# A one-column exponential on ScalarE ahead of each step's scores, in the second phase of a two-block transformer kernel

## The chip, the cores and the metric

The kernel runs on one core of one Trainium2 chip. The metric is the device time of one execution in microseconds (us). The kernel before was run three times: 3278.76, 3273.80 and 3276.89 us, with a median of 3276.89 us. One further execution was profiled.

The engines are named as in the profile: PE is TensorE's matmuls and PEld its weight loads, DVE is VectorE, ACT is ScalarE, POOL is GpSimd and SP is SyncE, which here only issues transfers.

## The reference, cut to what matters

The input is x of shape 8 x 1024 x 256 in float32. Two residual blocks follow each other; the second one has two layers.

```python
x = x + latent_attention(layernorm(x), ...)     # 16 heads, causal, rotary: first phase
x = x + local_blocks(layernorm(x), ...)         # second phase, DEPTH = 2 layers

# one layer of the second phase
h = shift_token(x)
q, k, v = split(h @ wqkv)                       # 8 heads of 64
q, k = rotary_xpos(l2norm(q) * qs, l2norm(k) * ksc)
x = x + softmax(window_mask(8 * q @ k.T)) @ v @ wo   # window 128: own block and the one before
h = layernorm(shift_token(x)) * lg + lb
a, g = split(h @ w1 + b1)                       # 682 columns each
x = x + (a * gelu(g)) @ w2 + b2
```

The scores need an exponential and the MLP needs a Gelu. Both are computed on ScalarE.

## The kernel before, in words

The first phase (`mla`) takes about the first 985 us and computes the latent attention of all 8 batches. It isn't touched by the change. The second phase (`local`) runs 16 passes, one for each layer and batch, layer 0 of all batches first. A pass consists of 8 windows of 128 tokens for the attention and of 2 chunks of 512 tokens for the MLP.

The second phase is a software pipeline written out by hand. The loop at line 1210 makes one step for each window, 128 of them and 11 more to drain. Inside `manual_schedule` each engine executes its instructions in the order in which the code issues them. In step s the loop issues, in this order:

- `both` of window s-4: the sums of masked exponentials of two blocks, on DVE.
- `qk` of window s: the projection to q and k on PE into a PSUM tile "pair" (line 892, recorded as L670 like all that goes through `times`), its squares on ACT (L897), and the rotary work on DVE and POOL (L899 to L912).
- `transposes` of window s-1: a transpose on DVE, a write to DRAM (z) and a read back into qkT through SP's queue (L930 to L939).
- `v` of window s: the projection to the values on PE ("pv", L670) and its eviction by ACT (L79).
- the first unit of the MLP (line 1227), from step 11 on.
- `values` of window s-4: the weighted values ("o", L1003) and the sums ("s", L1011) on PE, then the division on DVE.
- `scores` of window s-3: in two halves of four heads. Each half has its matmuls on PE into a "pair" tile (L962), an exponential of that tile on ACT (L968) into "pt", and masks on POOL (L970, L975).
- `output`, in every second step: the output projection on PE ("psw", L670).
- the second unit of the MLP (line 1238).

There are two "pair" tiles in PSUM, taken in turn (`turns`, line 869). A step takes three: one for `qk` and one for each half of the scores. The tile that `qk` of the next step writes is therefore the one that the first half's exponential of this step reads.

The MLP is a generator whose units the loop draws one at a time. A chunk has 8 units, so it spans 4 steps. Five units consist of a gate and a value projection ("ag", L670), a Gelu on ACT (L1127) and a product on DVE (L1128). The sixth does the remaining columns: half as many matmuls, a Gelu at L1137, and two products at L1142. The seventh is the down projection ("psy", L670), and the eighth only scales the next chunk's input on ACT (L1091). With two units a step the sixth is always the second unit of its step, and what follows it on PE is `qk` of the next step.

ScalarE keeps the table of one set of functions at a time, and exponential and Gelu belong to different sets. The compiler puts an ACT_TABLE_LOAD ahead of an activation that needs the other set; it is recorded under that activation's line. In the kernel before, the wait for PE that belongs to the first exponential of a step stands on the table load in 116 of its 120 cases. The other four are three loads without any wait, in the steps just after the change from layer 0 to layer 1, and one that waits for DVE, later on.

Of the kernel before, what the change touches and what calls it, by code (L numbers as in the profile page):

```python
# [29 lines left out]
F32 = mybir.dt.float32  # L30
F32R = mybir.dt.float32r
AF = mybir.ActivationFunctionType
# [4 lines left out]
P = 128  # L37
# [45 lines left out]
def preln_mla_local_kernel(  # L83
# [27 lines left out]
    nc = tc.nc  # L111
# [44 lines left out]
    def mla(ctx: ExitStack, verdict):  # L156
# [453 lines left out]
        ALONE = 1 + max(step for step, what in beside.items() for who, name, _ in what if who == 0 and not name.startswith("out"))  # L610
        E = mybir.EngineType
        line, done, turning = [], [], []
        with tc.manual_schedule(engines={E.PE, E.DVE, E.Activation, E.Pool}):
            for b in range(B + 1):
# [43 lines left out]
    def local(ctx: ExitStack, verdict):  # L658
# [4 lines left out]
        p1 = ctx.enter_context(tc.tile_pool(name="l1", bufs=1))  # L663
# [31 lines left out]
        def load_attention(l):  # L695


            w = {}
            queue = nc.sync if l else nc.scalar
            w["qkv"] = wa.tile([P, 2, 3 * INNER], F32, tag="qkv", name=f"l_qkv{l}")  # L700
            nc.sync.dma_start(w["qkv"], wqkv[l].rearrange("(c p) e -> p c e", p=P))

            for name, src in (("cos", xpos_cos), ("sin", xpos_sin)):
                w[name] = wa.tile([P, NT, 2, DH], F32, tag=name, name=f"l_{name}{l}")
                queue.dma_start(w[name], src)
                f = wa.tile([P, 2, DH], F32, tag=f"f{name}", name=f"l_f{name}{l}")
                for i, sc_ in enumerate((q_scale, k_scale)):
                    if name == "cos":
                        queue.dma_start(f[:, i, :], sc_[l].partition_broadcast(P))
                    else:  # L710
                        queue.dma_start(f[:, i, :H], sc_[l, H:].partition_broadcast(P))
                        queue.dma_start(f[:, i, H:], sc_[l, :H].partition_broadcast(P))
                w[f"f{name}"] = f
            return w

        def scale_tables(w):
            for name in ("cos", "sin"):
                f = w[f"f{name}"].unsqueeze(1).to_broadcast([P, NT, 2, DH])
                nc.vector.tensor_tensor(w[name], w[name], f, ALU.mult)

        def load_o(l):

            w = wa.tile([P, 4, D], F32, tag="o", name=f"l_o{l}")
            for g in range(2):
                for j in range(4):
                    h = 4 * g + j
                    nc.sync.dma_start(
                        w[32 * j : 32 * j + 32, 2 * g : 2 * g + 2],
                        wo[l, h * DH : (h + 1) * DH].rearrange("(a p) e -> p a e", a=2),
                    )  # L730
            return w
# [451 lines left out]
        windows = len(passes) * NT  # L1183
        streams = {}

        def ahead(n):
            if n < len(passes):
                l, b = passes[n]
                if n not in streams:
                    streams[n] = stream(b, l)  # L1190
                return next(streams[n])
# [10 lines left out]
        def each(step, name, back):  # L1202
            j = step - back
            if 0 <= j < windows:
                n, i = divmod(j, NT)
                getattr(made[n], name)(i)

        E = mybir.EngineType
        with tc.manual_schedule(engines={E.PE, E.DVE, E.Activation, E.Pool}):
            for step in range(windows + LAG):  # L1210
                n, i = divmod(step, NT)
                if step < windows and i == 0:
                    l, b = passes[n]
                    if n and b == 0:
                        o = w["o"]
                        w = load_attention(l)
                        w["o"] = o
                    made[n] = Pass(n, l, b, w, *ready.pop(n))
                late = step < windows and n and i == 0 and b == 0
                each(step, "both", 4)  # L1220
                if not late:
                    each(step, "qk", 0)
                each(step, "transposes", 1)
                if not late:
                    each(step, "v", 0)
                if step >= LAG:
                    next(units, None)
                if NT - 2 <= i and step < windows:
                    ahead(n + 1)
                each(step, "values", 4)  # L1230
                each(step, "scores", 3)
                j = step - 6
                if 0 <= j < windows and j % 2 == 0:
                    made[j // NT].output(j % NT // 2)
                elif 0 <= j < windows - 1 and (j + 1) % (B * NT) == 0:
                    w["o"] = load_o(passes[(j + 1) // NT][0])
                if step >= LAG - 2:
                    next(units, None)
                if late:
                    scale_tables(w)  # L1240
                    each(step, "qk", 0)
                    each(step, "v", 0)
                if i >= NT - 5 and step < windows:
                    got = ahead(n + 1)
                    if got:
                        ready[n + 1] = got
            for _ in units:
                pass
# [524 lines left out]
    with ExitStack() as two:  # L1773
        local(two, verdict)
# [4 lines left out]
    column = const.tile([P, 1], F32, name="column")  # L1779
# [84 lines left out]
```

## Time and profile before

| what | us |
|---|---|
| median of three runs | 3276.89 |
| the profiled execution, its own time | 3275.27 |
| its span, first to last instruction | 3273.5 |
| first phase, up to about | 985 |
| the second phase fills, about | 985 to 1120 |
| second phase, steady part | 1120 to 3195 |
| drain of the last chunks | 3195 to 3273.5 |

Busy time of the engines by stretch, in us:

| stretch | length | PE | DVE | ACT | POOL |
|---|---|---|---|---|---|
| first phase | 985.0 | 930.94 | 866.75 | 785.88 | 88.72 |
| filling | 135.0 | 109.26 | 110.76 | 38.76 | 103.43 |
| steady part | 2075.0 | 2067.54 | 1665.21 | 874.15 | 1147.22 |
| drain | 78.5 | 69.46 | 28.37 | 13.70 | 2.23 |

A row of the instruction groups reads: line, engine, operation, written tile, read tiles, shape, count, then the busy time and the mean of one in ns, then the idle time of the engine ahead of the group and what ended it. "issue" means that nothing that the profile shows was waited for. The end of a matmul is modelled, its start is recorded. In the weight loads' rows, idle time is usual: the loads come in groups of four, with 0.30 us between groups when matmuls of 512 columns run without a stop.

### The profile page before, as it was taken

The page shows a single profiled execution, that of the slowest core. Times are in us where ns is not written, and L with a number is a line of the kernel's source. Part 1 is how long each engine was busy: PE and PEld are TensorE (multiplying, and loading weights), DVE is VectorE, ACT ScalarE, POOL GpSimd, SP SyncE. Part 2 cuts the span into 40 slices and gives each one's busy share as a digit, 9 for nine tenths or more (in the row PEclk, how much of TensorE's full clock was granted, in tenths as well). Part 3 has the DMA queues.
Part 4 walks back from the last instruction along what each step waited for, and adds up shares of the span by engine and source line. Part 5 has one row for each costly group of instructions (what it writes and reads, how often), then busy time and mean ns, then how long its engine had stood idle before and what let it go on. Part 6 is the DMA issues. An engine that isn't in the chain of part 4 may idle for free.

```text
span 3273.5 us, 112729 instructions
## 1 busy us (share of the span) xinstructions
PE 3177.2 (97%) x50274; PEld 1456.0 (44%) x50274; DVE 2671.1 (82%) x3934; ACT 1712.5 (52%) x2055; POOL 1341.6 (41%) x1064
## 2 busy tenths in 40 slices
PE   7999999999987999999999999999999999999998
PEld 2434343443333445444445444444554444544454
DVE  4999989998987888887888877777877878787773
ACT  6888888888852343444443444444444444444441
POOL 1001000000018655565555555555555555555540
PEclk9999999999998999999999999999999999999999
DMA  4133223323333444544445445444544545454431
GB/s 128 43 95 85 56 75 78 85 53 81 98 98 104 108 129 118 142 111 122 131 115 135 120 131 144 120 130 142 144 131 130 133 122 134 134 140 126 114 106 59
DMA packets 389900, 364.21 MB, mean 111 GB/s; under 512 B 158703, under 2 KB 337310, under 8 KB 389278
## 3 DMA queue, kind: packets, MB, share of 16 engines
q1 hardware_dynamic: 387422, 354.51, 40.1%
q8 instruction: 397, 6.50, 0.8%
q10 hardware_dynamic: 1984, 2.41, 0.2%
q14 instruction: 97, 0.79, 0.1%
HBM read 165.96 MB, written 140.51 MB: 94 GB/s over the span
## 4 chain that ended last, share of the span: by engine, by line
PE 84%; DVE 6%; ACT 4%; DMA 3%; issue 2%; SPq 1%; POOL 0%; ACTq 0%; DVEq 0%; POOLq 0%
PE ag L670 17%; PE pair L670 13%; PE psy L670 9%; PE psw L670 7%; PE acc L488 7%; PE pv L670 6%; PE o L1003 6%; PE sc L455 5%; PE pair L962 4%; DVE pt L477 3%; PE s L1011 2%; PE psx L201 2%; PE psq L201 1%; PE psR L201 1%; ACT pt L463 1%
## 5 line engine op out<-in xcount | busy, mean ns | idle before, releaser
L477 DVE TENSOR_TENSOR pt<-pt,er 128x1024 f32<-128x1024 f32 x576 | 671.9, 1222 | 35.5 <-ACT pt L463 35.5
L670 PE MATMUL ag<-d,l 128*32 128x512 f32 x5632 | 639.8, 593 | 0.7 <-ACT d L1085 0.4
L906 POOL TENSOR_TENSOR t<-t,t 128x1024 f32<-128x1024 f32 x128 | 304.2, 2377 | 780.2 <-DVE t L902 780.2
L463 ACT ACTIVATE pt<-sc 128x1024 f32<-128x1024 f32 x576 | 561.0, 1032 | 115.4 <-PE sc L455 105.6
L968 ACT ACT_TABLE_LOAD x120 | 154.0, 1283 | 686.9 <-PE pair L962 686.8
L670 PE MATMUL pair<-l_qkv,xT 128*32 128x512 f32 x4096 | 468.3, 597 | 6.6 <-ACT pt L968 3.2
L126 POOL TENSOR_TENSOR rn<-ss,half 128x16 f32<-128x16 f32 x128 | 373.4, 2917 | 13.9
L488 PE MATMUL acc<-pt,v 128*32 128x512 f32 (+3 forms) x3072 | 345.6, 497 | 11.1 <-DVE pt L477 10.0
L670 PEld LDWEIGHTS ag<-d,l 128*32 128x32 f32 x5632 | 179.0, 110 | 384.0 <-issue 362.0
L897 ACT ACTIVATE sq<-pair 128x1024 f32<-128x1024 f32 x128 | 131.2, 1025 | 331.0 <-issue 256.0
L899 DVE TENSOR_TENSOR t<-pair,l_cos 128x1024 f32<-128x1024 f32 x128 | 156.3, 1221 | 155.1 <-ACT sq L897 154.8
L670 PE MATMUL psy<-l,hid 128*32 128x256 f32 x5120 | 282.1, 379 | 0.0
L670 PEld LDWEIGHTS pair<-l_qkv,xT 128*32 128x32 f32 x4096 | 132.6, 111 | 307.8 <-issue 252.5
L1128 DVE SCALAR_TENSOR_TENSOR hid<-ag,l_b,ge 128x512 f32<-128x512 f32 x160 | 115.9, 724 | 188.2 <-ACT ge L1127 164.5
L968 ACT ACTIVATE pt<-pair 128x1024 f32<-128x1024 f32 (+1 forms) x256 | 235.1, 969 | 56.4 <-PE pair L962 55.1
L912 POOL TENSOR_TENSOR t<-t,rn 128x1024 f32<-128x1024 f32 x128 | 245.4, 1918 | 10.0
L455 PE MATMUL sc<-q,k 32*128 32x512 f32 (+3 forms) x3072 | 245.2, 380 | 4.0 <-ACT pt L463 3.0
L1003 PEld LDWEIGHTS o<-pt,v 128*32 128x32 f32 x7680 | 212.8, 110 | 72.7 <-issue 68.9
L670 PE MATMUL pv<-l_qkv,xT 128*32 128x512 f32 x2048 | 244.1, 592 | 0.0
L670 PE MATMUL psw<-l_o,oT 128*32 128x256 f32 x4096 | 240.2, 386 | 0.1
L1003 PE MATMUL o<-pt,v 128*32 128x128 f32 x7680 | 235.6, 273 | 1.7 <-POOL pt L970 1.6
L420 POOL TENSOR_SCALAR_AFFINE_SELECT er<-er 128x128 f32<-128x128 f32 x64 | 39.1, 610 | 480.7 <-ACT er L418 480.7
(324 smaller groups left out, 4639.5 us busy)
## 6 DMA issues: line engine op xcount, KB each, us to landing
z<-turned SPq DMA_DIRECT2D x512, 128.0 KB, 2.8
qkT<-z SPq DMA_DIRECT2D x128, 512.0 KB, 3.9
y<-xs SPq DMA_DIRECT2D x128, 128.0 KB, 3.8
h<-y SPq DMA_DIRECT2D x32, 512.0 KB, 4.4
zx<-turneds SPq DMA_DIRECT2D x120, 128.0 KB, 2.8
xT<-zx SPq DMA_DIRECT2D x240, 64.0 KB, 2.9
zh<-turnedh SPq DMA_DIRECT2D x120, 128.0 KB, 2.3
d<-zh SPq DMA_DIRECT2D x30, 512.0 KB, 3.3
```

The source lines that it names most:

```text
L126: nc.gpsimd.tensor_tensor(out_, in_, half[:, :n], ALU.pow)
L455: nc.tensor.matmul(two[n // 2][:, n % 2, lo : lo + w], k[rows], q[rows, h], start=(h == 1), stop=(h == 0),)
L463: nc.scalar.activation(pt, sc, AF.Exp, scale=SCALE)
L477: nc.vector.tensor_tensor(t, t, er.to_broadcast([P, 1024 // w, w]), ALU.mult)
L488: nc.tensor.matmul(self.acc[g][32 * n : 32 * n + 32, q0 - c * 512 :], self.v[:, kb, h * VW : h * VW + 32], pts[n // 2][:, n % 2, lo : lo + w],
L670: nc.tensor.matmul(out[four], w[:, four], rhs, start=start, stop=stop)
L897: nc.scalar.activation(sq, qk, AF.Square)
L899: nc.vector.tensor_tensor(t1, qk, A[:, i].unsqueeze(2).to_broadcast([P, 2, HEADS, DH]), ALU.mult)
L906: nc.gpsimd.tensor_tensor(t1, t1, t2, ALU.add)
L912: nc.gpsimd.tensor_tensor(t1, t1, rn.unsqueeze(3).to_broadcast([P, 2, HEADS, DH]), ALU.mult)
L968: nc.scalar.activation(pt[:, :, : n * P], flat[:, :, : n * P], AF.Exp, scale=-1.0)
L1003: nc.tensor.matmul(o[32 * j : 32 * j + 32, g, a, :], vs[m][:, h * DH + a * 32 : h * DH + a * 32 + 32], pts[m][g][:, place(j), off : off + ...
```

## The change

Two tiles of one column are made ahead of the loop: `column`, which POOL sets to zero, and `spark`. In each step that has scores, a single ACT instruction is issued between the weighted values and the scores: the exponential of `column` into `spark`. Nothing reads `spark`.

```diff
@@ -1205,6 +1205,10 @@
                 n, i = divmod(j, NT)
                 getattr(made[n], name)(i)
 
+        column = p1.tile([P, 1], F32, name="column_l")
+        nc.gpsimd.memset(column, 0.0)
+        spark = p1.tile([P, 1], F32, name="spark")
+
         E = mybir.EngineType
         with tc.manual_schedule(engines={E.PE, E.DVE, E.Activation, E.Pool}):
             for step in range(windows + LAG):
@@ -1228,6 +1232,8 @@
                 if NT - 2 <= i and step < windows:
                     ahead(n + 1)
                 each(step, "values", 4)
+                if 0 <= step - 3 < windows:
+                    nc.scalar.activation(spark, column, AF.Exp)
                 each(step, "scores", 3)
                 j = step - 6
                 if 0 <= j < windows and j % 2 == 0:
```

## The prediction

> **What bounds the kernel now.** I read the page first, then the busy time by stretch, the chain of work that ended last around one chunk boundary, and the timelines of TensorE, its weight loads and ScalarE at two boundaries that differ in one thing.
>
> From the page: the busy shares, and the group that the change is about.
>
> ```profile
> PE 3177.2 (97%) x50274; PEld 1456.0 (44%) x50274; DVE 2671.1 (82%) x3934; ACT 1712.5 (52%) x2055; POOL 1341.6 (41%) x1064
> L968 ACT ACT_TABLE_LOAD x120 | 154.0, 1283 | 686.9 <-PE pair L962 686.8
> ```
>
> TensorE bounds the kernel. ScalarE loads the exponential's table 120 times, 1.28 us each, and nearly always it first sits idle until TensorE has finished the scores (686.8 us of waiting): the load comes after the wait, not during it. The busy time by stretch for the second phase's steady part (columns: stretch, its length, then busy time of PE, PEld, DVE, ACT, POOL, the granted clock and DMA):
>
> ```profile
> 1120.00:3195.00 2075.00, 2067.54 (x36870) 1000.66 (x36864) 1665.21 (x2628) 874.15 (x941) 1147.22 (x851) 1.00 0.47 127
> ```
>
> By this TensorE idles 7.5 us of 2075 us, but ends of matmuls are modelled, so a short stall can hide under a "busy" matmul. The chain shows one. At a chunk boundary (start, length, what):
>
> ```profile
> 1848.77 0.50 ACT L968
> 1849.27 0.79 issue
> 1850.06 1.03 ACT pt L968
> 1851.10 0.04 issue
> 1851.14 3.64 PE pair L670 x32
> ```
>
> The path leaves TensorE, goes through the load (0.50 + 0.79 = 1.29 us) and one exponential (1.03 us), and comes back to the next window's q and k. That matmul group writes the PSUM tile which the first exponential of the step before reads; there are two such tiles and three uses a step. What stands between is only the second half of the scores and whatever the MLP's second unit gives TensorE. In most steps that is 3.4 us or more. In the step with the small remainder unit it is 16 matmuls, and this is what happens (timeline of TensorE; start, length):
>
> ```profile
> 1849.09 1.92 PE L670 MATMUL ag<-d,l 128*32 128x512 f32 x16
> 1851.14 3.64 PE L670 MATMUL pair<-l_qkv,xT 128*32 128x512 f32 x32
> 1854.60 0.61 PE L670 MATMUL pv<-l_qkv,xT 128*32 128x512 f32 x4
> ```
>
> The profile holds a boundary without the late load. In one step just after the layer change the load carries no wait, so ScalarE did it right behind the Gelu, 2.65 us before the scores were ready:
>
> ```profile
> 2272.51 0.69 ACT L1127 ACTIVATE ge<-ag,l_b 128x512 f32<-128x512 f32 x1 [1.13 <-PE ag L670]
> 2273.22 1.28 ACT L968 ACT_TABLE_LOAD   x1
> 2277.16 1.94 ACT L968 ACTIVATE pt<-pair 128x1024 f32<-128x1024 f32 x2 [2.65 <-PE pair L962]
> ```
>
> and TensorE there, same unit, same order:
>
> ```profile
> 2277.52 1.92 PE L670 MATMUL ag<-d,l 128*32 128x512 f32 x16
> 2279.26 3.62 PE L670 MATMUL pair<-l_qkv,xT 128*32 128x512 f32 x32
> 2282.70 0.61 PE L670 MATMUL pv<-l_qkv,xT 128*32 128x512 f32 x4
> ```
>
> From the first remainder matmul to the first of the values' projection it is 5.51 us with the late load (1849.09 to 1854.60) and 5.18 us with the early one (2277.52 to 2282.70): 0.33 us, of which 0.31 is the stall and 0.02 the weight load that could not be pulled ahead. Is it kept? The down projections of successive chunks, by the timeline of TensorE:
>
> ```profile
> 1224.34 8.82 PE L670 MATMUL psy<-l,hid 128*32 128x256 f32 x160
> 1294.05 6.23 PE L670 MATMUL psy<-l,hid 128*32 128x256 f32 x112
> ...
> 2215.04 8.81 PE L670 MATMUL psy<-l,hid 128*32 128x256 f32 x160
> 2284.41 5.79 PE L670 MATMUL psy<-l,hid 128*32 128x256 f32 x104
> ```
>
> The chunk with the stall lasts 69.71 us and the one without 69.37 us. The 0.33 us was not handed back within the chunk.
>
> **What the Trainium skill says.** "ScalarE: Activation LUTs", section "What ACT_TABLE_LOAD costs", gives about 1283 ns for a load, which the trace repeats exactly, and a drain of about 1380 ns on top, which it does not show: the Gelu's load at 1852.02 starts 0.02 us after the exponential's end, and the exponential starts 11 ns after its load. I take 1.28 + 0.01 us. "Perfetto Trace Analysis", section "Tensor Engine Instruction (MATMUL, LD_WEIGHTS)", says the end of a TensorE instruction is an estimate; hence I count from start to start. "TensorE: Matmul & The Clock Gate", section "Step-by-step: what each phase is for", says weights are pulled ahead of running matmuls; here the early boundary loads them at 2278.84, 0.42 us ahead of their matmul, the late one at 1851.14 together with it.
>
> **The change part by part.** *The load moves.* The instruction order of the changed kernel has the same 120 exponential loads and 121 Gelu loads; the 120 stand ahead of the one-column exponential and carry no wait, and the wait for TensorE is on the first real exponential. No other engine's order changes, except for one more memset on POOL before the loop. So a load starts when ScalarE gets there: after the values' eviction or the first unit's Gelu. Apart from the four loads that ran early, the shortest idle time before a load is 3.1 us, so load and one-column exponential fit before the scores are ready in every step.
>
> *The cost of the one-column exponential.* No row has this shape. The rotary exponentials of line 418 take 293 ns for 128 columns and 617 ns for 512, that is 0.84 ns a column and 186 ns fixed: 0.19 us. The skill's ScalarE section gives the same 186 ns with immediate scale and bias. 128 of them are 24 us on an engine busy 874 of 2075 us, in idle stretches of at least 3.1 us: 0 us on the path. Eight come before the first Gelu and bring no load; ScalarE is busy 39 of 135 us there. Were the cover gone, 0.19 us in 28 steps would be 5 us. Its wait is for its own predecessor's write, a step earlier: nothing.
>
> *What is gained.* The first exponential ends about 1.3 us earlier. The stall was 0.33 us, so it goes whole: the chain would have the tile free at 1848.77 + 1.03 + 0.04 = 1849.84, while TensorE wants weights at about 1850.41 (one group of four 0.43 us after the load at 1849.98). 0.57 us to spare. Where such a boundary stands: 32 chunks, of which the last three have no later q and k: 29, less the early one: 28. The waits say the same:
>
> ```profile
> PEld pair L670 <- ACT pt L968: 37.0, 54, 1.3
> ```
>
> 54 waits in the steady part; an ordinary one between groups of four weight loads is 0.30 us and a stalled one 1.03: 1.03 n + 0.30 (54 - n) + 0.28 = 37.0 gives n = 28, where 0.28 is the surplus of one longer stall (1.31 us, at 2209.86). The sum: 27 x 0.33 + 0.60 = 9.5 us. Nothing in the other steps: with a full unit or an output projection between, TensorE does not wait for an exponential. The second Gelu of a step and the mask on POOL also come 1.3 us earlier, into engines that wait for others. What is late next: once, shortly before the layer change, TensorE waits 2.8 us for the q/k transfer, and that chain starts from TensorE's own output, so it moves along.
>
> Against its own time: span 3273.5 - 9.5 = 3264.0, and with the 1.8 us around it 3265.8. The profiled execution (3275.27) lies 1.6 us under the median, 3276.89; so 3267.4 us, -0.29%. I count 0.2% (6.6 us) as about what a measurement can tell from no change.
>
> **The rivals.** *The gain is handed back* (no change, 3275 to 3277): TensorE arrives 0.33 us earlier at something that has its own clock, a transfer or VectorE (busy 80% there). For it: VectorE's share. Against: the 69.37 us chunk. *The larger reading* (3256): the weight loads' idle is 1.03 instead of 0.30 us, so 0.73 x 28 = 20 us. Against: the loads are normally pulled ahead, so most of this is lost lead, and start to start it is 0.33. *Slower* (above 3283.5): every tile allocated later in the two working pools lies 64 bytes further on. If a q/k round trip got longer by this, the place is the 2.8 us wait and its like at the 15 changes of pass, where SyncE's queue holds the stream's transfers ahead; it decides from 9.5 + 6.6 = 16 us in all, 1.1 us a change. Against: every row keeps its length and size; unknown otherwise, so from 0 to 16 us, and I take 0. *It does not do what it says* (3277 to 3282): the exponential still starts 1.3 us behind the scores, 0 to 5 us lost to the extra instruction; the order of instructions speaks against it.
>
> **How the numbers follow.** Forecast 0.76, handed back or not working 0.14, larger 0.05, slower 0.05. The forecast itself spans 8.5 to 10 us of gain, and the three runs before span 5 us: 3264 to 3271. With a part of the handed-back case and of the larger one I take 3263 to 3274. Faster by over 0.2% (below 3270.3): nearly all of the first (0.71) and the larger case, 0.76; within 0.2%: 0.18; slower: 0.06.
>
> **What would show it.** Table loads on the new line, 120 of them, with no wait for TensorE, and no idle time left that is ended by TensorE ahead of a load of the exponential; the first remainder matmul to the first of the values' projection 5.18 us at every boundary; chunks of 69.37 and 70.5 instead of 69.7 and 70.86 us; the weight loads' wait for the exponentials near 8 us in place of 37.0. The prediction is wrong if these hold and the end does not move (handed back), if boundaries keep 5.5 us, or if the wait for the q/k transfer grows.

## The result, and the profile after

Over 16 runs of each kernel the changed kernel takes 3267.6 us (median; 3265.09 to 3272.61) and the kernel before 3275.38 us (3273.72 to 3279.6). The ratio is 0.9977, with a 95% interval of 0.9969 to 0.9984: 7.8 us faster, where 9.5 us were forecast. The interval reaches from 5.2 to 10.2 us, so the times alone can't tell these two apart; the traces below can. Two repeats beside other experiments gave 0.9979 (0.9970 to 0.9988) and 0.9981 (0.9974 to 0.9989).

The table loads, first. This is the view of instruction groups on ScalarE between 1120 and 3195 us of the changed kernel (busy time, mean ns, then the idle time ahead and what ended it):

```profile
L968 ACT ACTIVATE pt<-pair 128x1024 f32<-128x1024 f32 (+1 forms) x238 | 218.3, 968 | 523.6 <-PE pair L962 523.6
L1236 ACT ACT_TABLE_LOAD x119 | 152.7, 1283 | 2.1
L1236 ACT ACTIVATE spark<-column_l 128x1 f32<-128x1 f32 x119 | 24.1, 203 | 1.4
```

The wait for the scores is now ahead of the exponential. The loads, as many and as long as before, have 2.1 us of idle time ahead of them in all: they run when ScalarE gets there. At a chunk boundary it looks like this (timeline of ScalarE, changed kernel):

```profile
1844.72 0.69 ACT L1127 ACTIVATE ge<-ag,l_b 128x512 f32<-128x512 f32 x1 [1.13 <-PE ag L670]
1845.43 1.28 ACT L1236 ACT_TABLE_LOAD   x1
1846.72 0.20 ACT L1236 ACTIVATE spark<-column_l 128x1 f32<-128x1 f32 x1
1849.43 1.02 ACT L968 ACTIVATE pt<-pair 128x1024 f32<-128x1024 f32 x1 [2.50 <-PE pair L962]
```

and on TensorE:

```profile
1849.73 1.92 PE L670 MATMUL ag<-d,l 128*32 128x512 f32 x16
1851.48 3.62 PE L670 MATMUL pair<-l_qkv,xT 128*32 128x512 f32 x32
1854.91 1.90 PE L670 MATMUL pv<-l_qkv,xT 128*32 128x512 f32 x16
```

ScalarE has 2.50 us left over after load and extra exponential. From the remainder unit's first matmul to the first of the values' projection it is 5.18 us, where the kernel before had 5.51. By the same starts it is 5.17 to 5.18 us at all 29 boundaries of the changed kernel; before, it was 5.51 us at 27 of them, 5.79 at one and 5.17 at the early one. The weight loads' wait for the exponentials, 37.0 us in the steady part before, is gone there; over the whole program this remains:

```profile
PEld pair L670 <- ACT pt L968: 4.6, 4, 2.2
```

all of it in the filling stretch, before the first unit of the MLP, when no such unit lies between the scores and the next q and k.

Then the chunks, each taken from the first matmul of one down projection to that of the next. Here are three successive down projections in layer 0 (timeline of TensorE, changed kernel):

```profile
1226.27 8.82 PE L670 MATMUL psy<-l,hid 128*32 128x256 f32 x160
1295.64 8.82 PE L670 MATMUL psy<-l,hid 128*32 128x256 f32 x160
1366.50 3.85 PE L670 MATMUL psy<-l,hid 128*32 128x256 f32 x68
```

One chunk lasts 69.37 us, 0.34 less than the same chunk before. The other lasts 70.86 us, as long as before; the same two down projections in the kernel before:

```profile
1294.05 8.82 PE L670 MATMUL psy<-l,hid 128*32 128x256 f32 x160
1364.91 8.82 PE L670 MATMUL psy<-l,hid 128*32 128x256 f32 x160
```

In layer 1 both kinds are shorter where nothing else delays them (69.71 to 69.37, 70.79 to 70.46). So in six chunks of layer 0 the gain was handed back, and the profile names the place. TensorE and VectorE in the second chunk, changed kernel:

```profile
1307.73 1.35 PE L962 MATMUL pair<-qkT 64*32 64x160 f32 x64
1309.38 2.99 PE L670 MATMUL psw<-l_o,oT 128*32 128x256 f32 x49 [0.30 <-DVE xs L1165]
```

```profile
1306.22 1.32 DVE L909 TENSOR_SCALAR ss<-ss 128x16 f32<-128x16 f32 x1
1307.46 1.29 DVE L930 STREAM_TRANSPOSE turned<-t 128x512 f32<-128x512 f32 x2
1308.68 1.24 DVE L1165 TENSOR_TENSOR xs<-psy,xs 128x512 f32<-128x512 f32 x2
1309.86 1.04 DVE L794 TENSOR_SCALAR xs<-xs,mvs,rstds 128x256 f32<-128x256 f32 x3
```

The output projection (psw) needs a PSUM bank, of which the pool has three in turn; the down projection's is the next one, and VectorE frees it with the first addition at L1165. No row on VectorE shows an idle time ahead: it works without a gap from the step's beginning (the rows between 1291 and 1311 us follow each other at 0.035 us or less). In these steps it also normalises the stream of a later pass (the row of L794), which the program does in layer 0 alone; that this is what fills VectorE is read from the rows and was not tried.

Before the change TensorE came to this point just ahead of VectorE. Its output projection began 1.32 us after the scores, and begins 1.65 us after them now:

```profile
1306.14 1.32 PE L962 MATMUL pair<-qkT 64*32 64x160 f32 x64
1307.46 3.66 PE L670 MATMUL psw<-l_o,oT 128*32 128x256 f32 x64
```

The waits for L1165 over the whole program (total us, times, longest), the first row from the kernel before, the other two from the changed one:

```profile
PEld psw L670 <- DVE xs L1165: 1.9, 6, 0.3
PEld psw L670 <- DVE xs L1165: 3.9, 6, 0.7
PE psw L670 <- DVE xs L1165: 1.9, 6, 0.3
```

So the projection's weight loads waited for VectorE in the same six places before, 0.32 us each. TensorE now comes 0.33 us earlier, and they wait 0.33 us longer.

### The profile page after: what moved, and what is told of

It is laid out like the page before. It is cut to its first block, busy times and chain, and to the rows that moved or that the text cites. A ratio compares the mean times of both kernels' runs of the same rounds, so it can differ in the third digit from the quotient of the medians.

```text
span 3267.4 us, 112857 instructions
## 1 busy us (share of the span) xinstructions
PE 3171.2 (97%) x50274; PEld 1460.1 (45%) x50274; DVE 2673.8 (82%) x3934; ACT 1734.9 (53%) x2183; POOL 1341.1 (41%) x1065
## 4 chain that ended last, share of the span: by engine, by line
PE 56%; DVE 4%; issue 1%; DMA 0%; SPq 0%; ACT 0%; DVEq 0%
PE ag L670 16%; PE pair L670 11%; PE psy L670 7%; PE psw L670 6%; PE pv L670 5%; PE o L1003 5%; PE pair L962 4%; PE s L1011 1%; DVE turned L930 0%; DVE rs L1015 0%; DVE bnsts L783 0%; DVE t L902 0%; DVE both L987 0%; DVE turnedh L804 0%; SPq L850 0%
## 5 line engine op out<-in xcount | busy, mean ns | idle before, releaser
L1015 DVE RECIPROCAL rs<-s 128x256 f32<-128x256 f32 x128 | 222.8, 1741 | 13.0 <-PE s L1011 13.0
```

The lines of the kernel that those rows point to most:

```text
L1015: nc.vector.reciprocal(rs, s)
```

## The experiments

Each is compared with the kernel before, run on the same chip in the same rounds. Chunk lengths are worked out from the starts of down projections, as above.

**Only the boundaries.** The instruction is issued in the remainder steps alone:

```diff
-                if 0 <= step - 3 < windows:
+                if 0 <= step - 3 < windows and step >= LAG and step % 4 == 1:
                     nc.scalar.activation(spark, column, AF.Exp)
```

> The one-column exponential is issued only in the steps whose second MLP unit is the small remainder unit (steps 13, 17, ... 129: 30 instead of 128); everywhere else the table load stays behind the scores. Theory (only the 28 boundaries with 16 matmuls of cover mattered): the whole gain, 7.8 us below before, and chunks of 69.37 us in layer 0; some 90 loads with the wait for TensorE stay and cost nothing. Rival (earlier exponentials help in every step, through POOL's masks or VectorE's products): a third or less of the gain, below 3 us.

Measured: 3270.66 against 3277.82 us, ratio 0.9980 (0.9974 to 0.9987). Undisturbed chunks are 69.37 and 70.46 us (70.86 in layer 0), as in the changed kernel. The late loads are still there in numbers (waits of this kernel: total us, times, longest):

```profile
ACT L968 <- PE pair L962: 569.6, 87, 12.2
```

87 loads behind the scores, and the gain is 7.2 us against the changed kernel's 7.8, which the intervals don't tell apart. The boundaries carry the gain.

**All but the boundaries.** The part of the condition that the last experiment added, negated.

> The opposite half: the one-column exponential in every step with scores except the remainder steps. Theory: the stalls of 0.33 us at 28 boundaries stay, chunks of 69.7 and 70.86 us, 0 us against before (within 1.5 us). Rival (gain in all steps): 5 us or more below before.

Measured: 3278.0 against 3277.82 us, ratio 1.0000 (0.9992 to 1.0009), chunks of 69.71 and 70.86 us in layer 0. Its waits for the exponentials and for L1165:

```profile
PEld pair L670 <- ACT pt L968: 31.4, 31, 1.0
PEld psw L670 <- DVE xs L1165: 1.9, 6, 0.3
```

The stalls are there, and the six waits for L1165 are as short as in the kernel before. The 98 extra exponentials and 90 early loads change nothing. With the first experiment this settles where the gain is.

**An instruction without a table.** `AF.Identity` in place of `AF.Exp`; the one-column tile is then copied instead of exponentiated, and nothing reads it.

> The same one-column instruction in the same place, but an identity, which needs no table of its own: the load stays with the first real exponential of each step. It has the same tiles, so the same shift of the later tiles by 64 bytes, and the same count of instructions. Theory (the place of the load is all there is): 0 us against before, within 1.5 us, 116 loads with their wait for TensorE, 0.33 us stalls. Rival (the shift of the tiles, or the order of waits on ScalarE, made the gain): the gain of 7.8 us stays. If the instruction itself cost time on the path: up to 5 us above before.

Measured: 3278.8 against 3277.82 us, ratio 1.0003 (0.9994 to 1.0011). Its waits:

```profile
ACT L968 <- PE pair L962: 674.3, 116, 12.0
PEld pair L670 <- ACT pt L968: 42.0, 59, 2.6
```

These are nearly the rows of the kernel before (686.8 us, 116 times; 41.6 us, 59 times). The program makes the same tiles in the same order and as many instructions as in the changed kernel, so it is the place of the load that counts.

**How much cover there is.** Eight exponentials in place of one, and then twenty in the remainder steps and one elsewhere:

```diff
                 if 0 <= step - 3 < windows:
-                    nc.scalar.activation(spark, column, AF.Exp)
+                    for _ in range(8):          # second kernel: 20 if step >= LAG and step % 4 == 1 else 1
+                        nc.scalar.activation(spark, column, AF.Exp)
```

> Eight one-column exponentials in place of one, 0.2 to 0.26 us each[...], where the shortest idle stretch is 3.1 us and 4.0 us at the boundaries that stall. Theory (the cost is hidden while it fits, and the boundary has 0.57 us to spare): the time of the changed kernel within 1.5 us. Rival (the instruction costs something on the path each time): 0.2 us x 7 x 28 = 39 us or more above.

> The changed kernel with 20 one-column exponentials, 0.235 us from start to start, in the remainder steps, and one in the others. Load and exponentials take 1.29 + 4.70 = 5.99 us, the idle stretch ahead of the scores is 4.00 us: the first real exponential starts 1.99 us late, where the kernel before had it 1.29 us late. Theory (TensorE has 0.99 us of cover from the scores' readiness and loses what is beyond it): a stall of 1.0 us at 29 boundaries, 29 us in all, so 18 to 20 us above before, chunks of 70.4 and 71.5 us in place of 69.37 and 70.46. Rival (the stall is not set by the first exponential): much less, near the changed kernel.

Measured with eight: 3269.99 against 3278.31 us, ratio 0.9976 (0.9967 to 0.9986), the changed kernel's time. Load and exponentials take about 3.1 us there (0.235 us from start to start) and are fully hidden. With twenty: 3295.63 against 3277.81 us, ratio 1.0053 (1.0038 to 1.0069), that is 17.8 us above before, just under the 18 to 20 that were expected. Timelines of ScalarE and TensorE at one of its boundaries:

```profile
1853.69 4.66 ACT L1237 ACTIVATE spark<-column_l 128x1 f32<-128x1 f32 x20
1858.26 1.92 ACT L968 ACTIVATE pt<-pair 128x1024 f32<-128x1024 f32 x2
```

```profile
1856.70 1.92 PE L670 MATMUL ag<-d,l 128*32 128x512 f32 x16
1859.31 3.64 PE L670 MATMUL pair<-l_qkv,xT 128*32 128x512 f32 x32 [0.69 <-ACT pt L968]
```

From remainder to q and k it is 2.61 us, and 1.75 in the changed kernel; the chunks are 70.27 and 71.36 us, 0.90 us longer than 69.37 and 70.46. 29 boundaries at 0.90 us are 26 us, less the 9.5 us that the late load had cost: 16.6 us, and 17.8 was measured, with an interval from 12.5 to 22.6. The profile puts TensorE's wait down to this exponential, as it does the weight loads' wait in the kernel before, and not to the Gelu or the mask that move along with it. The first real exponential starts 1.9 us late here, 1.3 us late in the kernel before, and 0.90 and 0.33 us are lost. From these two points, about 1 us of lateness is covered at this place, and each microsecond beyond it costs one.

**The handed-back part.** In the steps with the down projection as their first unit, q and k's transposes are issued behind it, so that the additions at L1165 come first on VectorE:

```diff
-                each(step, "transposes", 1)
+                down = step >= LAG and step % 4 == 2
+                if not down:
+                    each(step, "transposes", 1)
                 if not late:
                     each(step, "v", 0)
                 if step >= LAG:
                     next(units, None)
+                if down:
+                    each(step, "transposes", 1)
```

> The changed kernel, and in steps whose first MLP unit is the down projection, the transposes of q and k (1.29 us on VectorE) are issued after that unit instead of before it, so that VectorE's additions of the down projection (L1165) come 1.24 us earlier. Theory (in layer 0 every second chunk gave its 0.33 us back, since the output projection then waits for a PSUM bank that these additions free, VectorE being busy without a gap): the waits of TensorE's output projection for L1165 are gone, the six chunks of 70.86 us become 70.53 us, 2 us below the changed kernel, 9.5 to 10 us below before. Rival (VectorE has no time to give, something else of its queue is then late): no gain over the changed kernel. Risk: the q/k transfer starts 1.2 us later, and its one visible wait before the layer change grows by up to 1.2 us.

Measured: 3268.79 against 3277.82 us, ratio 0.9976 (0.9967 to 0.9986): 9.0 us, where 9.5 to 10 were expected. No matmul of the projection waits for L1165 any more, and the six chunks are 70.46 us. Its weight loads still show the wait, but shorter than in the kernel before, 0.25 us each:

```profile
PEld psw L670 <- DVE xs L1165: 1.5, 6, 0.3
```

Beside the changed kernel on one chip, it was this:

> The changed kernel once more, beside the same runs of the kernel before as the next ones. Theory: 7.5 us below before (28 boundaries less 6 that hand their 0.33 us to VectorE).

> The changed kernel with the transposes of q and k after the down projection's unit, again, beside the changed kernel. Theory: 2 to 2.4 us below the changed kernel (6 chunks of layer 0, 70.86 to 70.46 us), 9.5 to 10 us below before. Rival: the later q/k transfer gives it back elsewhere: no difference.

The medians are 3270.22 us for the changed kernel and 3270.13 for the reordered one, ratios 0.9979 (0.9970 to 0.9988) and 0.9972 (0.9962 to 0.9982): not told apart, though the six chunks are again 70.46 us. The wait for the q/k transfer before the layer change is 2.6 and 2.8 us in the two reordered traces, and 2.0 to 2.5 us in the three of the changed kernel. In both reordered traces one chunk after the layer change became 70.8 us instead of 69.37: TensorE pauses within an output projection, and the profile gives no releaser ("issue"). In the first of them:

```profile
2223.19 3.22 PE L670 MATMUL psw<-l_o,oT 128*32 128x256 f32 x55
2227.43 0.81 PE L670 MATMUL psw<-l_o,oT 128*32 128x256 f32 x9 [1.01 <-issue]
```

The idle time shown is 1.0 us behind a modelled end; the chunk is 1.4 us longer. The reordering without the exponential, on the kernel before:

> The kernel before with only this reordering, without the one-column exponential. Theory: TensorE there does not wait for L1165 yet, or by 0.07 us at most in six chunks (70.86 against 70.79 us in layer 1): below 1 us of gain, so the two edits together give more than their sum. Rival (the reordering is a gain of its own): 2 us or more.

Measured: 3279.02 against 3278.31 us, ratio 1.0003 (0.9995 to 1.0012). Its layer 0 chunks are 70.79 instead of 70.86 us, as expected, and it too has a long chunk (70.63 us) after the layer change. VectorE's order was worth 0.07 us a chunk before, too little to see in the times; it is worth 0.40 us a chunk once the late table load is gone. Since the reordering pays in layer 0 alone, the last version restricts it:

```diff
-                down = step >= LAG and step % 4 == 2
+                down = LAG <= step < windows // DEPTH and step % 4 == 2
```

> The changed kernel, with the transposes of q and k after the down projection's unit in the steps of layer 0 alone, where the changed kernel waits for L1165. In layer 1 the same order gained nothing, and one chunk there became 1.4 us longer in each reordered kernel. Theory: six chunks of 70.46 us, no chunk of 70.7 us or more right after the layer change, 2.4 us below the changed kernel, 9.5 to 10 us below before. Rival: the 1.4 us pause appears at another place.

> The changed kernel beside the two above: 7.5 us below before, six waits for L1165.

Measured: 3268.22 against 3277.81 us, ratio 0.9970 (0.9959 to 0.9981), beside 3272.28 us and 0.9981 (0.9974 to 0.9989) for the changed kernel, 5.5 us below before where 7.5 were expected. TensorE and VectorE in the place where the changed kernel waited:

```profile
1307.08 1.32 PE L962 MATMUL pair<-qkT 64*32 64x160 f32 x64
1308.33 3.66 PE L670 MATMUL psw<-l_o,oT 128*32 128x256 f32 x64
```

```profile
1306.83 1.27 DVE L1165 TENSOR_TENSOR xs<-psy,xs 128x512 f32<-128x512 f32 x2
1308.03 1.29 DVE L930 STREAM_TRANSPOSE turned<-t 128x512 f32<-128x512 f32 x2
```

The output projection follows the scores after 1.25 us, and 1.65 us in the changed kernel; both additions end 0.2 us before it. The six chunks are 70.46 us and the pause after the layer change is absent. A shorter one, 0.4 us of idle time in an output projection at 2084 us, is in this trace and not in the first of the changed kernel; a later trace of the changed kernel has one of 0.6 us at that place too. A repeat:

> The version with the reordering in layer 0 alone, again, since one comparison did not part it from the changed kernel. Theory: 9.5 us below before, a ratio near 0.997, six chunks of 70.46 us. Rival: the earlier 0.997 was luck, and the ratio is the changed kernel's 0.998.

gave 3267.7 against 3275.76 us, ratio 0.9975 (0.9965 to 0.9984): 8.1 us, where 9.5 were expected. The traces show 6 x 0.40 = 2.4 us less in the six chunks, and both ratios lie below the three of the changed kernel, but the intervals overlap, and other chunks vary by as much from trace to trace. That the six chunks are shorter is shown; that the kernel is faster than the changed kernel is not.

## Why the prediction was right, and where it was off

**The load moves and is hidden: right.** 120 loads on the new line, none waiting for TensorE. The identity experiment shows no effect of anything else in the edit.

**The extra exponential costs nothing on the path: right.** It measures 203 ns where 190 were taken from the row of line 418. The fixed part of 186 ns, which the prediction took from that row and found in a page too, is thus a little low for one column; the measurement decides. Eight of them still cost nothing.

**0.33 us a boundary, 28 boundaries: right.** The reading by starts held: 5.18 us at the boundaries, and the last experiments show the loss growing with lateness beyond a fixed cover. The larger reading, 0.73 us each from the weight loads' idle time (a forecast of 3256 us), is out: the stretch shrank by 0.33 us. The weight loads' wait for the exponentials was expected near 8 us and went to nothing in the steady part: besides the stalls, the ordinary pauses between groups of loads are no longer put down to an exponential either.

**"Nothing in the other steps": right**, by the two halves of the first experiments.

**"The 0.33 us was not handed back": the term that was off.** It was taken from the one boundary with an early load, and this one lies in layer 1. In every second chunk of layer 0 VectorE has no idle time, and six chunks of 70.86 us stayed as they were, where 70.5 had been expected. The sum with that term is 9.5 - 6 x 0.33 = 7.5 us, and 7.8 us was measured. That the forecast time, 3267.4 us, lies 0.2 us from the measured 3267.6 is luck: the kernel before came out at 3275.38 us over 16 runs and not at the 3276.89 us of three, and this made up for the smaller gain. The rival "handed back" named VectorE as the place, and it was so in 6 of 28 boundaries. The trace of before held two signs that I did not use: the same chunk took 70.86 us in layer 0 and 70.79 us in layer 1, and the projection's weight loads already waited for L1165 six times. TensorE was thus already held up by 0.07 us there and had nothing to gain by coming earlier.

**Slower through the moved tiles, or through a longer wait for the q/k transfer: not so.** The identity experiment makes the same tiles and has the time of before. TensorE's waits for that transfer are 14.6 us in all in the profile before and 12.6, 4.7 and 18.0 us in the three traces of the changed kernel, so one trace of each says little; the one ahead of the layer change is 2.8 us before and 2.0, 2.3 and 2.5 us in these three.

What stays open is the pauses of TensorE, up to 1.4 us, for which the profile gives no releaser. Most traces show one or more. Why one of 1.3 to 1.4 us kept its place in all three traces of the kernels reordered in both layers was not tried. Executions differ in other places too: the chunk across the layer change lasts 75.1 to 79.1 us in the fourteen traces, 76.7 in the one before and 75.1, 76.8 and 77.5 in the three of the changed kernel. Within one kernel the runs mostly spread over 5 to 12 us, which is why the account above rests on stretches that repeat and not on whole times.

## What to carry to other kernels

In this kernel a table load sat where its activation sits and, in 116 of 120 cases, took over that activation's wait; a tiny activation of the same function, with no wait for another engine, moved the load into the idle time ahead. It is worth something only where the activation's result is wanted back soon: here in 28 of 120 places, and 30 extra instructions did what 128 did. Count such a stall from the starts of matmuls at a place with it and one without, and check the second place in every phase of the loop: where another engine ran without a gap, as VectorE did in six chunks here, the gain ended at that engine. A wait that the profile before already shows there is the sign to look for.

## What was not expected of the hardware

One-column exponentials that follow each other start every 0.235 us while each is recorded with 0.203 us, so a row of them costs more than their busy time. All of them write the same tile, so each waits for the one before it; other tiles were not tried. And a reordering on VectorE that shows no gain alone (ratio 1.0003) took 0.40 us off each of six chunks once ScalarE's late load was out of the way.
